# Output products of a batch put together in a fused diffusion, attention, expert and low-rank kernel, with a rebuilt start and waits tile by tile

## The chip, the core and the metric

The kernel runs on one core of a Trainium2 chip. The metric is the device time of one execution in microseconds (us), as the median of several runs. The core has a matrix engine (TensorE, PE in the profile; PEld is its loading of the stationary operand), a vector engine (VectorE, DVE), a scalar engine (ScalarE, ACT), a general engine (GpSimd, POOL) and a queue that issues most transfers (SyncE, SP). Each engine works through its own list of instructions in order, and waits on semaphores for the others. SBUF is the working memory of 128 partitions; PSUM holds the results of TensorE, in banks of 128 x 512 values (the kernel lays out eight).

## What is computed

Eight batches of 512 x 512 values go through four layers. All is float32.

```python
x = diffuse(x, A, B, dt)       # L0: max(f + df * dt, 0); df from first and second
                               #     differences of A*f and B*f, one-sided at the borders
x = attention_block(x, ...)    # L1: layernorm scaled by an embedding of the time step,
                               #     16 heads of 32, with a bias and a mask; then an MLP of 2048
x = expert_ffn(x, eidx)        # L2: weights of the expert eidx[b]: gelu MLP, + x, layernorm,
                               #     * gamma[e] + beta[e]
feats = (x @ basis) @ basis.T[:, :32]
strength = sigmoid(relu(mean(x) @ gate_w1.T + gate_b1) @ gate_w2.T + gate_b2) * sigmoid(safety)
out = x + strength * (feats @ resp_w.T + resp_b + safety_bias)     # L3
```

## The kernel before

`fused_kernel` (L40) runs three stages one after another. P = 128 is the number of partitions, R = 4 the number of row groups of a batch (a batch is held as 128 partitions x 4 rows x 512), and RK = 32 the rank of L3. Instructions wrapped in `pin` keep the order of the program text on their engine, so this order is written out by hand.

**The grid stage** (`grid_stage`, L215 to L517) computes L0 of batch 0, and the border values ("edges") of all batches. At the start `rows_in` loads A, B and x in half blocks on the SP queue (L274). Then SP issues the weights of the embedding (`load_wada`), Wq, Wk, Wv and Wo (`load_w`, L168) and the small bias rows (`load_rows`). VectorE multiplies coefficients with x (ca, cb, cc, ce, cg, then e, g, c, ga, gb, q, t, all at L237); TensorE adds the shifted products up in four accumulators l, by multiplying with shifted identity matrices zi (L243). POOL brings in the border rows: `edge_in` issues, behind a copy of x named gate_e (L312), transfers of edge_f into fe (64 partitions) and, per side, a broadcast of edge_c into ec, eight broadcasts in all. The coefficients also go to DRAM as coef_q, coef_e and so on (L386), for the other batches. Then come the embedding product pe on TensorE (L148), the row blocks x = relu(l * dth + f) for r = 0, 3, 1, 2, and after all four the transfers x<-xe that put the border values of batch 0 in place (two on SP, two on ACT). The statistics ln_st of the layernorm (L499) follow, for rows 0 and 3 after those transfers; the normalised x (L511) and the scale ada (L157) release the next stage.

**The attention stage** (`attention_stage`, L521 to L1105) goes through 128 units (b, c, r): batch, group of four heads, row group. Its start, before the loop, is at L1042 to L1065: loads of masks (`mask_in`: mu, L564), of biases (`load_bias`: bt) and of the next batch's grid data (`grid_loads`: gf, gq), the transposes of x (`x1_in`: xtr, L546), the products pq (L543), `grid_early` (gq times gf on VectorE, L663), the products pk and pv, and the scores s (L543). The scores of four heads lie on four groups of 32 rows of TensorE, and go to four banks. The grid of batches 1 to 7 is computed by VectorE inside the loop.

**The MLP stage** (`mlp_stage`, L1109 to L1769) makes 16 passes q: 0 to 7 the MLP of L1, 8 to 15 the experts. A pass has its products cut in a Strassen-like way: 4 groups of 7 products u with the first weights, at steps 0 to 27, then 7 products y with the second weights that begin at steps 28, 32, 36, 40, 44, 48 and 52 and take 4 steps each. `at(hooks, s, f, ...)` runs f behind step s; so all other work is threaded in by hand. All matmuls of this stage have the line of a helper, L1137; additions on VectorE have L1143, those on POOL L1146.

In passes 9 to 15 the batch before (o = q - 1) gets its L3: `tail_norm` at step 8, `tail_turn` at 29 to 35, `tail_gamma` 37, `tail_feats` 38, `gate` 39, `strength` 41, `add_beta` 42 (x + beta on POOL), and `tail_out` for the four row groups r behind steps 49, 51, 53 and 55 (50 to 53 in pass 15):

```python
def tail_sum(q, r):                       # L1643
    po = ps.tile([P, D], F32, tag="u" if last else "tr", bufs=6 if last else 2)
    mm(po, ft[m, :], rw[m, :], True, not last)      # m: rows 32r to 32r+31
def tail_add(q, r):                       # L1653
    # x[:, r] = po * strength + x[:, r] on VectorE (L1656); behind odd r the store to out
```

Row group r of po stands on TensorE's rows 32r to 32r + 31. PSUM tiles come from two sets: "u", six banks, for the products u and y, and "tr", two banks, for transposes and small products. The last batch (o = 15) has its L3 after the loop (L1741 to L1769), with its four po one after another in the text, in the set "u".

A pool of tiles (`tile_pool`) that is opened where a closed pool has lain waits at its first use for what used that memory before. All pools of the kernel are opened without an option for this.

Of the kernel before, what the change touches and what calls it, by code (L numbers as in the profile page):

```python
# [11 lines left out]
F32 = mybir.dt.float32  # L12
# [12 lines left out]
R = 4  # L25
# [14 lines left out]
def fused_kernel(ctx: ExitStack, tc: tile.TileContext, a: dict):  # L40
# [64 lines left out]
    freq = ep.tile([P, 2], F32, name="freq")  # L105
    nc.scalar.dma_start(freq, a["c_freq"])
    bada = ep.tile([P, 2 * KC], F32, name="bada")
    nc.scalar.dma_start(bada, a["b_ada"])
    nc.scalar.dma_start(sigs, a["safety"][None, :].to_broadcast([P, NB]))
    nc.scalar.dma_start(eidx, a["eidx"][None, :])  # L110
    nc.vector.tensor_scalar(bada[:, 0:KC], bada[:, 0:KC], 1.0, None, ALU.add)
    tf = ep.tile([P, NB], F32, name="tf")
# [25 lines left out]
    nc.scalar.activation(sc, sc, AF.Silu)  # L138
    nc.scalar.activation(sigs, sigs, AF.Sigmoid)

    def embed(ps):
# [11 lines left out]
        return pe  # L153

    def embed_out(pe):
        tc.keep_in_program_order(
            nc.vector.tensor_tensor(  # L157
                ada, pe, bada[:, :, None].to_broadcast([P, 2 * KC, NB]), ALU.add
            )
        )  # L160
# [3 lines left out]

    def load_w():
        for n in ("Wq", "Wk", "Wv", "Wo"):
            w[n] = w8(wo8, n)
            nc.sync.dma_start(w[n], a[n].rearrange("(k p) m -> p k m", p=P))  # L168

# [3 lines left out]

    def load_rows():
        nc.sync.dma_start(bqk[:, 0, :], a["bq"])
# [4 lines left out]
    grid = grid_stage(  # L180
        tc, a, const, small, dram, xt[0], mhalf, ident, load_wada, load_w, load_rows, embed,
        embed_out,
    )


    io = ctx.enter_context(tc.tile_pool(name="io", bufs=1))
    g2 = const.tile([P, 2, KC], F32, name="g2")
    nc.scalar.dma_start(g2[:, 0, :], a["g2"])
    nc.scalar.dma_start(g2[:, 1, :], a["beta2"])
    b1 = const.tile([P, NJ], F32, name="b1")  # L190
    nc.scalar.dma_start(b1, a["b1"])
    wl3 = const.tile([P, KC, RK], F32, name="wl3")
    x1d = [dram.tile([P, R, D], F32, name=f"x1d_{b}") for b in range(NB)]
    first = attention_stage(
        tc, a, small, xp, xt, x_home, x1d, grid, ident, sc1, shift, io, wo8, w, (bqk, bvc, bo),
        g2, mhalf,
    )
# [17 lines left out]
def grid_stage(  # L215
    tc, a, const, small, dram, x, mhalf, ident, load_wada, load_w, load_rows, embed,
    embed_out,
):
# [26 lines left out]
    with ExitStack() as ctx:  # L245
# [21 lines left out]
        ec = gp.tile([N, 12, W + 2], F32, name="ec")  # L267
        pin(nc.gpsimd.memset(ec, 0.0))
        pin(nc.gpsimd.memset(fe, 0.0))
# [6 lines left out]
        with tc.tile_pool(name="raw", bufs=1) as rp:  # L276
# [3 lines left out]

            def edge_in(i, k):
                lo, hi = max(0, W * k - 1), min(D, W * k + W + 1)
                u = slice(lo - W * k + 1, hi - W * k + 1)
                p0 = n * i
                pin(nc.gpsimd.dma_start(fe[p0 : p0 + n, :, u], a["edge_f"][:, :, lo:hi]))
                for side in range(2):
                    p1 = p0 + side * NB
                    pin(
                        nc.gpsimd.dma_start(
                            ec[p1 : p1 + NB, :, u],  # L290
                            a["edge_c"][side : side + 1, :, lo:hi].to_broadcast([NB, 12, hi - lo]),
                        )
                    )

# [7 lines left out]
            rows_in(b2, a["B"][2])  # L302
            nc.scalar.dma_start(gw, a["c_ghost"].to_broadcast([P, 16]))
            nc.scalar.dma_start(dth, a["dt"][None, :].to_broadcast([P, NB]))
            load_wada()
            load_w()
            load_rows()
# [5 lines left out]
            for i, k in enumerate(blocks):  # L313
                edge_in(i, k)

# [9 lines left out]

        wp = ctx.enter_context(tc.tile_pool(name="l0", bufs=1))
        acc = [ps.tile([P, D], F32, name=f"l0_{r}") for r in range(R)]
# [53 lines left out]
        for m, w, o in (  # L381
            ("q", b2, 1), ("e", ce, 1), ("c", cc, 0), ("g", cg, 1), ("a", ca, 0), ("b", cb, 0)
        ):
# [92 lines left out]
        pin(nc.vector.tensor_scalar(xe, xe, 0.0, None, ALU.max))  # L476
        xed = dram.tile([n, D], F32, name="xed")
        for i, k in enumerate(blocks):
            pin(nc.gpsimd.dma_start(xed[:, W * k : W * k + W], xe[n * i : n * i + n, :]))
        pe = embed(ps)  # L480
        pin(nc.vector.tensor_scalar(dth, dth, 0.5, None, ALU.mult))
        st = small.tile([P, R, 6], F32, name="ln0_st", tag="ln0_st", bufs=1)
        mv = small.tile([P, R, 2], F32, name="ln0_mv", tag="ln0_mv", bufs=1)
        for r in (0, 3, 1, 2):
            stt(x[:, r, :], acc[r], dth[:, 0:1], f[:, r, :], ALU.mult, ALU.add)
            pin(nc.scalar.activation(x[:, r, :], x[:, r, :], AF.Relu))
        for o, u, c in ((0, 3 * n, 0), (n, n, 2 * W)):
            for side, q_ in ((0, nc.sync), (1, nc.scalar)):
                p, r = side * (P - 1), side * (R - 1)
                e0 = o + side * NB  # L490
                pin(
                    q_.dma_start(
                        x[p : p + 1, r, c : c + 2 * W].rearrange("o (b w) -> o b w", w=W),
                        xe[e0 : e0 + u + 1 : u, :],
                    )
                )

# [23 lines left out]
def attention_stage(  # L521
    tc, a, small, xp, xt, x_home, x1d, grid, ident, sc1, shift, io, wo8, w, rows,
    g2, mhalf,
):
# [10 lines left out]
    with ExitStack() as ctx:  # L535
        wp = ctx.enter_context(tc.tile_pool(name="aw", bufs=1))
        pp = ctx.enter_context(tc.tile_pool(name="ap", bufs=2))
        ps = ctx.enter_context(tc.tile_pool(name="a_ps", bufs=1, space=PSUM))

# [340 lines left out]
        def grid_early(j):  # L880
            grid_sums(1, j)
            grid_loads(1, j)
# [163 lines left out]
        grid_loads(1, -2)  # L1046
        load_bias(*units[0])
        grid_loads(1, -1)
        mask_in(0, 1)
        load_bias(*units[1])  # L1050
        for c in range(KC):
            x1_in(0, c)
        mask_out(0, 0)
        pin(nc.scalar.copy(bvr, bvc[:, :, None].to_broadcast([P, KC, P])))
        add_mask(*units[0])
        drain(q_block(0, 0))
        grid_early(0)
        grid_early(1)
# [3 lines left out]
        mask_in(0, 2)  # L1062
        mask_in(0, 3)
        grid_early(2)
        scores(*units[0])  # L1065
# [43 lines left out]
def mlp_stage(tc, a, small, xp, io, wo8, x1d, ident, eidx, sigs, layernorm, rstd_of, phalf, wl3, g2, b1, first):  # L1109
# [19 lines left out]
    with ExitStack() as ctx:  # L1129
        wp = ctx.enter_context(tc.tile_pool(name="fw", bufs=1))  # L1130
        ap = ctx.enter_context(tc.tile_pool(name="fa", bufs=2))
        ps = ctx.enter_context(tc.tile_pool(name="f_ps", bufs=2, space=PSUM))
        dp = ctx.enter_context(tc.tile_pool(name="x2_dram", bufs=1, space=bass.MemoryType.DRAM))
# [509 lines left out]
        def tail_sum(q, r):  # L1643
            last = q == NQ - 1
            ft, m = outs[q]["ft"], slice(r * RK, (r + 1) * RK)
            po = outs[q]["po", r] = ps.tile(
                [P, D], F32, name=f"po_{q}_{r}", tag="u" if last else "tr", bufs=6 if last else 2
            )
            mm(po, ft[m, :], rw[m, :], True, not last)
            if last:  # L1650
                mm(po, ones[m, :], rb[m, :], False, True)

        def tail_add(q, r):  # L1653
# [6 lines left out]
            if r % 2:  # L1660
# [21 lines left out]
        for q in range(NQ):  # L1682
# [36 lines left out]
            elif q > NB:  # L1719
# [138 lines left out]
```

## Time and profile before

| | us |
|---|---|
| median of 3 runs | 2807.26 (2805.81 to 2810.29) |
| profiled execution | 2809.32 |
| its span | 2807.5 |
| VectorE busy | 1942.0 |
| ScalarE busy | 1002.8 |
| GpSimd busy | 1503.9 |
| software queue q0 (POOL's transfers) | 3680 packets, 11.07 MB |

The span is what the profile covers; the execution's own time is 1.8 us longer. The mean granted clock of TensorE is 0.991 of full speed. The grid stage with the start of attention takes about the first 80 us; the attention loop goes on to 1143 us, and the MLP stage to the end.

How to read the profile: "y<-wo,act" is an instruction by the names of its output and inputs; "L1137" is its line in the kernel; "128x512 f32" is its shape and type. "x16" counts instructions. The chain is followed back from the last instruction of a window: each piece is a stretch of work, or a transfer, that released the next. A line of waits tells which engine's instruction waited for whose. A float32 matmul shows as two or four instructions, one for each pass.

### The profile page before, as it was taken

To read this page: it belongs to the slowest core of one execution; us is meant where nothing else is said; L and a number is where in the kernel's file an instruction comes from. 1 tells how busy PE (TensorE), PEld (TensorE's weight loads), DVE (VectorE), ACT (ScalarE), POOL (GpSimd) and SP (SyncE) were. 2 spreads that over 40 slices of the span, in tenths; PEclk is the share of its full clock that TensorE was granted. 3 is DMA by queue.
4 is the path that set the end of the run, shared out by engine and by line. 5 is a ranking of instruction groups with operands and counts; after the bars stand their busy time and mean duration, and the time that the engine had idled before them with its cause. 6 is when DMAs were issued, how large, how long until landed. Compare 5 with 4: busy or idle time off the path is not lost.

```text
span 2807.5 us, 39790 instructions
## 1 busy us (share of the span) xinstructions
PE 2729.1 (97%) x14654; PEld 2011.6 (72%) x14654; DVE 1942.0 (69%) x3581; ACT 1002.8 (36%) x2133; POOL 1503.9 (54%) x1081
## 2 busy tenths in 40 slices
PE   5999999999999998999999999999999999999998
PEld 3455555555555554788888888888888888888886
DVE  6888898988888766576666756655466556556554
ACT  1466666666666666212111211211121121121221
POOL 3455555555555654466566655656456545535633
PEclk9999999999999999999999999999999999999998
DMA  9665657566666554542533444253223133143120
GB/s 300 225 204 180 235 172 241 186 223 214 194 233 191 157 160 158 181 121 49 158 124 83 109 143 124 49 169 120 73 97 125 59 137 128 42 154 113 42 75 31
DMA packets 190400, 405.62 MB, mean 144 GB/s; under 512 B 24104, under 2 KB 28784, under 8 KB 183934
## 3 DMA queue, kind: packets, MB, share of 16 engines
q1 hardware_dynamic: 185192, 391.93, 42.2%
q0 software_dynamic: 3680, 11.07, 3.2%
q8 instruction: 117, 1.92, 0.3%
q14 instruction: 77, 0.63, 0.1%
q10 hardware_dynamic: 1334, 0.07, 0.0%
HBM read 367.32 MB, written 31.50 MB: 142 GB/s over the span
## 4 chain that ended last, share of the span: by engine, by line
PE 86%; DVE 9%; ACT 2%; DMA 2%; issue 1%; SPq 0%; DVEq 0%; ACTq 0%; POOL 0%
PE y L1137 28%; PE u L1137 28%; PE tr L546 6%; PE s L543 4%; PE ctx L543 4%; PE o L543 3%; PE pv L543 3%; PE pq L543 3%; PE pk L543 2%; DVE bt L973 2%; DVE x L663 2%; DVE pt L998 1%; DMA Wo<-in_Wo 1%; ACT bt L978 1%; PE po L1137 1%; PE btr L1140 1%
## 5 line engine op out<-in xcount | busy, mean ns | idle before, releaser
L1137 PE MATMUL y<-wo,act 128*128 128x256 f32 x2560 | 578.9, 381 | 0.0
L950 POOL TENSOR_TENSOR bt<-bt,mk 128x1024 f32<-128x1024 f32 x256 | 543.2, 2142 | 64.2 <-DMA bt<-in_bias 61.2
L1137 PEld LDWEIGHTS y<-wo,act 128*128 128x128 f32 x2560 | 479.4, 190 | 82.2 <-issue 20.6
L978 ACT ACTIVATE bt<-bt,mn 128x512 f32<-128x512 f32 x512 | 365.4, 715 | 115.5 <-DVE mn L973 115.4
L546 PEld LDWEIGHTS tr<-ident,bt 128*128 128x128 f32 x2048 | 228.2, 141 | 167.7 <-issue 115.7
L1137 PE MATMUL u<-bt,wi 128*128 128x256 f32 x1440 | 330.5, 379 | 0.0
L973 DVE CUSTOM_DVE_ANT_0 bt<-s,bt 128x512 f32<-128x512 f32 x512 | 330.4, 682 | 0.0
L1143 DVE TENSOR_TENSOR act<-u,u 128x512 f32<-128x512 f32 x256 | 173.3, 686 | 209.9 <-PE u L1137 132.6
L1137 PEld LDWEIGHTS u<-bt,wi 128*128 128x128 f32 x1440 | 273.5, 190 | 37.2
L546 PE MATMUL tr<-ident,bt 128*128 128x128 f32 x2048 | 279.9, 278 | 18.8 <-DVE pt L998 7.7
L998 DVE COPY pt<-tr 128x512 f32<-128x512 f32 x256 | 175.8, 687 | 113.3 <-PE tr L546 113.0
L1137 PE MATMUL u<-tb,ws 128*128 128x256 f32 x1024 | 242.1, 379 | 0.0
L1137 PE MATMUL y<-t,s 128*128 128x256 f32 x1024 | 234.2, 380 | 0.0
L1000 ACT COPY pt<-tr 128x512 f32<-128x512 f32 x256 | 148.1, 579 | 183.1 <-PE tr L546 180.7
L1137 PEld LDWEIGHTS u<-tb,ws 128*128 128x128 f32 x1024 | 194.4, 190 | 26.5
L1146 POOL TENSOR_TENSOR t<-wo,t 128x512 f32<-128x512 f32 x64 | 104.5, 1647 | 200.5 <-PE y L1137 200.5
L1137 PEld LDWEIGHTS y<-t,s 128*128 128x128 f32 x1024 | 191.1, 190 | 24.1
L1457 ACT ACTIVATE act<-act,b 128x512 f32<-128x512 f32 x128 | 82.9, 711 | 292.4 <-DVE act L1143 292.4
L1457 ACT ACTIVATE act<-act,bi 128x512 f32<-128x512 f32 x128 | 83.8, 713 | 282.6 <-DVE act L1143 282.6
L1143 DVE TENSOR_TENSOR x<-y,x 128x512 f32<-128x512 f32 x96 | 64.5, 685 | 159.0 <-PE y L1137 105.1
L543 PE MATMUL s<-kt,qt 32*128 32x512 f32 x1024 | 171.7, 645 | 2.3 <-DVE mn L973 1.4
L1143 DVE TENSOR_TENSOR u<-u,u 128x512 f32<-128x512 f32 x192 | 131.3, 684 | 58.8 <-PE u L1137 58.8
(314 smaller groups left out, 4283.5 us busy)
## 6 DMA issues: line engine op xcount, KB each, us to landing
bt<-in_bias SPq DMA_DIRECT2D x256, 512.0 KB
wo<-in_W SPq DMA_DIRECT2D x32, 1024.0 KB
wi<-in_Wi SPq DMA_DIRECT2D x32, 1024.0 KB
wo<-in_Wo_e SPq DMA_DIRECT2D x32, 1024.0 KB
wi<-in_W SPq DMA_DIRECT2D x28, 1024.0 KB
gq<-coef_q SPq DMA_DIRECT2D x21, 512.0 KB
x1d<-x SPq DMA_DIRECT2D x8, 1024.0 KB
x<-x1d SPq DMA_DIRECT2D x8, 1024.0 KB
```

Source lines behind the costliest of these rows:

```text
L543: pin(nc.tensor.matmul(out, lhsT=lhsT, rhs=rhs, start=start, stop=stop))
L546: pin(nc.tensor.transpose(out, src, ident))
L663: pin(nc.vector.tensor_tensor(out, x, y, op))
L950: nc.gpsimd.tensor_tensor(bt, bt, mask[b, r][:, None, :].to_broadcast([P, 2, S]), ALU.add)
L973: nc.vector.tensor_tensor_reduce(bt[:, i, :], ss[h], bt[:, i, :], -1.0, 3.0e38, ALU.add, ALU.min, mn)
L978: nc.scalar.activation(bt[:, i, :], bt[:, i, :], AF.Exp, bias=mn, scale=-1.0, accum_out=sums[b, c, r][:, h : h + 1],)
L998: pin(nc.vector.tensor_copy(pt[:, :, r % 2, :], tr))
L1000: pin(nc.scalar.copy(pt[:, :, r % 2, :], tr))
L1137: pin(nc.tensor.matmul(out, lhsT=lhsT, rhs=rhs, start=start, stop=stop))
L1143: pin(nc.vector.tensor_tensor(out, x, y, op))
L1146: pin(nc.gpsimd.tensor_tensor(out, x, y, op))
L1457: nc.scalar.activation(acts[g][:, k, :], acts[g][:, k, :], func, bias=bi[:, j : j + 1])
```

## The change

Three things change.

*The tail.* po always takes a bank of the set "u". `tail_out` is gone; in passes 9 to 15 all four `tail_sum` run behind step 45, and the four `tail_add` behind steps 47, 48, 49 and 51.

*The start.* The edge coefficients come by four small transfers into a tile of 8 partitions (ec8), issued first on POOL; four matmuls with a selector (sel8) spread them to 64 partitions in PSUM, and ACT copies them to ec. Small loads (b_ada, eidx, gw, dth, safety) move from the ACT queue to SP, g2, beta2 and b1 to a later place on SP; the sigmoid of safety comes first on ACT. Of the attention weights only Wq and Wk are loaded early; Wv goes behind the first unit's bias, Wo behind the second's. The addition of 1 to b_ada goes behind the embedding product. The transfers x<-xe are issued behind row blocks 0 and 3, and those of xed move from POOL to the ACT queue. The store order of coef_c and coef_g is swapped. `grid_early(0)` stands ahead of the first `mask_out`, `add_mask` and `q_block`.

*The pools.* Eight pools (io, l0, aw, ap, a_ps, fw, fa, f_ps) get `reuse_waits="tile"`: the wait for what lay in the memory before is made for each tile by itself.

```diff
-                [P, D], F32, name=f"po_{q}_{r}", tag="u" if last else "tr", bufs=6 if last else 2
+                [P, D], F32, name=f"po_{q}_{r}", tag="u", bufs=6
-        def tail_out(q, rows):
-            for r in rows:
-                tail_sum(q, r)
-                tail_add(q, r)
...
                 for r in range(R):
-                    at(hooks, (50 + r) if q == NQ - 1 else (49 + 2 * r), tail_out, o, [r])
+                    at(hooks, 45, tail_sum, o, r)
+                    at(hooks, (47, 48, 49, 51)[r], tail_add, o, r)
```

```diff
+            for i, k in enumerate(blocks):
+                c, u = edge_cols(k)
+                pin(nc.gpsimd.dma_start(ec8[2 * i : 2 * i + 2, :, u], a["edge_c"][:, :, c]))
+            pin(nc.gpsimd.tensor_copy(
+                sel8, ident[0 : N // NB, 0 : N // NB, None].to_broadcast([N // NB, N // NB, NB])))
...
-            load_w()
+            load_w("Wq", "Wk")
...
             for i, k in enumerate(blocks):
-                edge_in(i, k)
+                c, u = edge_cols(k)
+                pin(nc.gpsimd.dma_start(fe[n * i : n * i + n, :, u], a["edge_f"][:, :, c]))
+            for i in range(4):
+                pec = ps.tile([N, 3, W + 2], F32, name=f"pec_{i}", tag="pec", bufs=2)
+                mm(pec, sel8.rearrange("q s b -> q (s b)"), ec8[:, 3 * i : 3 * i + 3, :], True, True)
+                pin(nc.scalar.copy(ec[:, 3 * i : 3 * i + 3, :], pec))
...
-        wp = ctx.enter_context(tc.tile_pool(name="l0", bufs=1))
+        wp = ctx.enter_context(tc.tile_pool(name="l0", bufs=1, reuse_waits="tile"))
...
         pe = embed(ps)
+        embed_bias()
...
         for r in (0, 3, 1, 2):
             stt(x[:, r, :], acc[r], dth[:, 0:1], f[:, r, :], ALU.mult, ALU.add)
             pin(nc.scalar.activation(x[:, r, :], x[:, r, :], AF.Relu))
-        for o, u, c in ((0, 3 * n, 0), (n, n, 2 * W)):
...
+            if r == 3:
+                edges()
+        xed = dram.tile([n, D], F32, name="xed")
+        for i, k in enumerate(blocks):
+            pin(nc.scalar.dma_start(xed[:, W * k : W * k + W], xe[n * i : n * i + n, :]))
```

```diff
         load_bias(*units[0])
+        load_w("Wv")
         grid_loads(1, -1)
         mask_in(0, 1)
         load_bias(*units[1])
+        load_w("Wo")
         for c in range(KC):
             x1_in(0, c)
+        grid_early(0)
         mask_out(0, 0)
         pin(nc.scalar.copy(bvr, bvc[:, :, None].to_broadcast([P, KC, P])))
         add_mask(*units[0])
         drain(q_block(0, 0))
-        grid_early(0)
```

More of the change, by code (lines that the diff above doesn't have):

```diff
@@ L106, in fused_kernel @@
     nc.scalar.dma_start(freq, a["c_freq"])
+    nc.sync.dma_start(sigs, a["safety"][None, :].to_broadcast([P, NB]))
+    nc.scalar.activation(sigs, sigs, AF.Sigmoid)
     bada = ep.tile([P, 2 * KC], F32, name="bada")
[L108 to L111, printed above, removed]
     tf = ep.tile([P, NB], F32, name="tf")
@@ L138, in fused_kernel @@
     nc.scalar.activation(sc, sc, AF.Silu)
-    nc.scalar.activation(sigs, sigs, AF.Sigmoid)
     def embed(ps):
@@ L153, in embed, with embed_bias @@
         return pe
+    def embed_bias():
+        tc.keep_in_program_order(
+            nc.vector.tensor_scalar(bada[:, 0:KC], bada[:, 0:KC], 1.0, None, ALU.add)
+        )
     def embed_out(pe):
@@ L163, in fused_kernel, with load_w @@
     w = {}
-    def load_w():
-        for n in ("Wq", "Wk", "Wv", "Wo"):
+    def load_w(*names):
+        for n in names:
             w[n] = w8(wo8, n)
-            nc.sync.dma_start(w[n], a[n].rearrange("(k p) m -> p k m", p=P))
+            tc.keep_in_program_order(
+                nc.sync.dma_start(w[n], a[n].rearrange("(k p) m -> p k m", p=P))
+            )
     bqk = const.tile([P, 2, KC], F32, name="bqk")
@@ L174, in load_rows @@
     def load_rows():
+        nc.sync.dma_start(bada, a["b_ada"])
+        nc.sync.dma_start(eidx, a["eidx"][None, :])
         nc.sync.dma_start(bqk[:, 0, :], a["bq"])
@@ L181, in fused_kernel, with load_late @@
         tc, a, const, small, dram, xt[0], mhalf, ident, load_wada, load_w, load_rows, embed,
-        embed_out,
+        embed_bias, embed_out,
     )
-    io = ctx.enter_context(tc.tile_pool(name="io", bufs=1))
+    io = ctx.enter_context(tc.tile_pool(name="io", bufs=1, reuse_waits="tile"))
     g2 = const.tile([P, 2, KC], F32, name="g2")
-    nc.scalar.dma_start(g2[:, 0, :], a["g2"])
-    nc.scalar.dma_start(g2[:, 1, :], a["beta2"])
     b1 = const.tile([P, NJ], F32, name="b1")
-    nc.scalar.dma_start(b1, a["b1"])
+    def load_late():
+        for t, v in ((g2[:, 0, :], "g2"), (g2[:, 1, :], "beta2"), (b1, "b1")):
+            tc.keep_in_program_order(nc.sync.dma_start(t, a[v]))
     wl3 = const.tile([P, KC, RK], F32, name="wl3")
@@ L195, in fused_kernel @@
         tc, a, small, xp, xt, x_home, x1d, grid, ident, sc1, shift, io, wo8, w, (bqk, bvc, bo),
-        g2, mhalf,
+        g2, mhalf, load_w, load_late,
     )
@@ L216, in grid_stage @@
     tc, a, const, small, dram, x, mhalf, ident, load_wada, load_w, load_rows, embed,
-    embed_out,
+    embed_bias, embed_out,
 ):
@@ L267, in grid_stage @@
         ec = gp.tile([N, 12, W + 2], F32, name="ec")
-        pin(nc.gpsimd.memset(ec, 0.0))
         pin(nc.gpsimd.memset(fe, 0.0))
@@ L279, in grid_stage, with edge_cols @@
             )
-            def edge_in(i, k):
+            ec8 = rp.tile([N // NB, 12, W + 2], F32, name="ec8")
+            sel8 = rp.tile([N // NB, N // NB, NB], F32, name="sel8")
+            pin(nc.gpsimd.memset(ec8, 0.0))
+            def edge_cols(k):
                 lo, hi = max(0, W * k - 1), min(D, W * k + W + 1)
[L283 to L293, printed above, removed]
+                return slice(lo, hi), slice(lo - W * k + 1, hi - W * k + 1)
+            for i, k in enumerate(blocks):
+                c, u = edge_cols(k)
+                pin(nc.gpsimd.dma_start(ec8[2 * i : 2 * i + 2, :, u], a["edge_c"][:, :, c]))
+            pin(
+                nc.gpsimd.tensor_copy(
+                    sel8, ident[0 : N // NB, 0 : N // NB, None].to_broadcast([N // NB, N // NB, NB])
+                )
+            )
             halves = slice(0, 2), slice(2, 4)
@@ L302, in grid_stage @@
             rows_in(b2, a["B"][2])
-            nc.scalar.dma_start(gw, a["c_ghost"].to_broadcast([P, 16]))
-            nc.scalar.dma_start(dth, a["dt"][None, :].to_broadcast([P, NB]))
+            nc.sync.dma_start(gw, a["c_ghost"].to_broadcast([P, 16]))
+            nc.sync.dma_start(dth, a["dt"][None, :].to_broadcast([P, NB]))
             load_wada()
-            load_w()
+            load_w("Wq", "Wk")
             load_rows()
@@ L313, in grid_stage @@
             for i, k in enumerate(blocks):
-                edge_in(i, k)
+                c, u = edge_cols(k)
+                pin(nc.gpsimd.dma_start(fe[n * i : n * i + n, :, u], a["edge_f"][:, :, c]))
+            for i in range(4):
+                pec = ps.tile([N, 3, W + 2], F32, name=f"pec_{i}", tag="pec", bufs=2)
+                mm(
+                    pec, sel8.rearrange("q s b -> q (s b)"), ec8[:, 3 * i : 3 * i + 3, :],
+                    True, True,
+                )
+                pin(nc.scalar.copy(ec[:, 3 * i : 3 * i + 3, :], pec))
             for h in halves:
@@ L381, in grid_stage @@
         for m, w, o in (
-            ("q", b2, 1), ("e", ce, 1), ("c", cc, 0), ("g", cg, 1), ("a", ca, 0), ("b", cb, 0)
+            ("q", b2, 1), ("e", ce, 1), ("g", cg, 1), ("c", cc, 0), ("a", ca, 0), ("b", cb, 0)
         ):
@@ L476, in grid_stage @@
         pin(nc.vector.tensor_scalar(xe, xe, 0.0, None, ALU.max))
-        xed = dram.tile([n, D], F32, name="xed")
-        for i, k in enumerate(blocks):
-            pin(nc.gpsimd.dma_start(xed[:, W * k : W * k + W], xe[n * i : n * i + n, :]))
         pe = embed(ps)
+        embed_bias()
         pin(nc.vector.tensor_scalar(dth, dth, 0.5, None, ALU.mult))
@@ L483, in grid_stage, with edges @@
         mv = small.tile([P, R, 2], F32, name="ln0_mv", tag="ln0_mv", bufs=1)
+        def edges():
+            for o, u, c in ((0, 3 * n, 0), (n, n, 2 * W)):
+                for side, q_ in ((0, nc.sync), (1, nc.scalar)):
+                    p, r = side * (P - 1), side * (R - 1)
+                    e0 = o + side * NB
+                    pin(
+                        q_.dma_start(
+                            x[p : p + 1, r, c : c + 2 * W].rearrange("o (b w) -> o b w", w=W),
+                            xe[e0 : e0 + u + 1 : u, :],
+                        )
+                    )
         for r in (0, 3, 1, 2):
@@ L486, in grid_stage @@
             pin(nc.scalar.activation(x[:, r, :], x[:, r, :], AF.Relu))
-        for o, u, c in ((0, 3 * n, 0), (n, n, 2 * W)):
[L488 to L496, printed above, removed]
+            if r == 3:
[3 more added lines that the diff above has]
+            pin(nc.scalar.dma_start(xed[:, W * k : W * k + W], xe[n * i : n * i + n, :]))
         def stats(r):
@@ L522, in attention_stage @@
     tc, a, small, xp, xt, x_home, x1d, grid, ident, sc1, shift, io, wo8, w, rows,
-    g2, mhalf,
+    g2, mhalf, load_w, load_late,
 ):
@@ L535, in attention_stage @@
     with ExitStack() as ctx:
-        wp = ctx.enter_context(tc.tile_pool(name="aw", bufs=1))
-        pp = ctx.enter_context(tc.tile_pool(name="ap", bufs=2))
-        ps = ctx.enter_context(tc.tile_pool(name="a_ps", bufs=1, space=PSUM))
+        wp = ctx.enter_context(tc.tile_pool(name="aw", bufs=1, reuse_waits="tile"))
+        pp = ctx.enter_context(tc.tile_pool(name="ap", bufs=2, reuse_waits="tile"))
+        ps = ctx.enter_context(tc.tile_pool(name="a_ps", bufs=1, space=PSUM, reuse_waits="tile"))
         pin = tc.keep_in_program_order
@@ L1063, in attention_stage @@
         mask_in(0, 3)
+        load_late()
         grid_early(2)
@@ L1129, in mlp_stage @@
     with ExitStack() as ctx:
-        wp = ctx.enter_context(tc.tile_pool(name="fw", bufs=1))
-        ap = ctx.enter_context(tc.tile_pool(name="fa", bufs=2))
-        ps = ctx.enter_context(tc.tile_pool(name="f_ps", bufs=2, space=PSUM))
+        wp = ctx.enter_context(tc.tile_pool(name="fw", bufs=1, reuse_waits="tile"))
+        ap = ctx.enter_context(tc.tile_pool(name="fa", bufs=2, reuse_waits="tile"))
+        ps = ctx.enter_context(tc.tile_pool(name="f_ps", bufs=2, space=PSUM, reuse_waits="tile"))
         dp = ctx.enter_context(tc.tile_pool(name="x2_dram", bufs=1, space=bass.MemoryType.DRAM))
```

## The prediction

> **What bounds the kernel now.** I read the page's busy shares and chain first. The chain is the path that ended last, and TensorE (PE) holds 86% of it:
>
> ```profile
> PE 2729.1 (97%) x14654; PEld 2011.6 (72%) x14654; DVE 1942.0 (69%) x3581; ACT 1002.8 (36%) x2133; POOL 1503.9 (54%) x1081
> PE 86%; DVE 9%; ACT 2%; DMA 2%; issue 1%; SPq 0%; DVEq 0%; ACTq 0%; POOL 0%
> ```
>
> So a microsecond leaves in two ways only: less TensorE work, or TensorE not waiting. The change tries one of each, and I read one view for each. First the chain of waits in pass q=12 (start, length, work):
>
> ```profile
> 2441.92 3.46 PE y L1137 x16
> 2445.38 1.05 PE po L1137 x2
> 2446.43 3.65 PE y L1137 x16
> 2450.08 1.05 PE po L1137 x2
> ```
>
> TensorE has no gap here. An output product po (two matmuls on 32 rows) takes 1.05 us, and the sixteen y behind it take 3.65 instead of 3.46 us: 1.05 + 0.19 = 1.24 (single starts give 1.248). Four stand in each of seven passes.
>
> Second the chain through the first 78 us, cut to its long pieces:
>
> ```profile
> 26.67 34.86 DMA Wo<-in_Wo
> ...
> 61.56 3.29 DMA x<-xe
> ...
> 65.32 3.54 DMA gf<-in_x
> 68.86 0.91 DVE x L511 x2
> ...
> 70.00 3.42 PE xtr L546 x16
> 73.42 3.45 PE pq L543 x8
> ...
> 77.56 4.28 DVE gq L663 x2
> ```
>
> Here transfers hold the end. The list of waits has the same from the engines (total, times, longest):
>
> ```profile
> PE l L243 <- DVE e L237: 26.6, 1, 26.6
> DVE ln_st L499 <- DMA x<-xe: 7.6, 1, 7.6
> PE xtr L546 <- DVE ada L157: 6.6, 1, 6.6
> DVE qe L237 <- DMA ec<-in_edge_c: 1.6, 1, 1.6
> DVE ca L237 <- DMA a<-in_A: 1.0, 1, 1.0
> ```
>
> TensorE waits 26.6 us for its first operand, works without a gap to 63.4 (timeline), then waits 6.6 us for a layernorm, whose last rows come by the edge transfers x<-xe.
>
> **The tail.** All four po of a batch move behind step 45, their adds to steps 47 to 51. Nothing is taken from the arithmetic; the question is whether four po cost four times one. Where row groups lie side by side, the timeline has (start, length, group):
>
> ```profile
> 81.07 1.14 PE L543 MATMUL s<-kt,qt 32*128 32x512 f32 x8 [0.78 <-ACT kt L632]
> 82.14 14.00 PE L543 MATMUL pv<-Wv,x 128*128 128x512 f32 x32
> ```
>
> Eight matmuls, the same size as po's, four row groups in four banks: the next work starts 1.07 us later. Four po would thus cost what one costs, plus 0.02. The last batch has its po together already, 1.87 us start to start for eight, at half clock: the same. Here the Trainium skill speaks a little against it: "TensorE: Matmul & The Clock Gate", Part 3, Measured speedup, gives a packing of four row groups 3.07 times, not 4. By that a group costs 4 × 1.05 / 3.07 = 1.37 us, by the row 1.07; over seven passes 2 us. I take the row, and leave the 2 us to the range. Saving per pass: 3 × 1.248 − 0.02 = 3.72. Passes 9 to 14: 6 × 3.72 = 22.3. In pass 15 one of the four bothers little work behind it (4.85 us for the four, 1.27 after; 3.6), and its split tail_norm has three adds put ahead of it on VectorE; its first transposes at step 51 have 3 us of room for 2.5 us, so I take off 0.3: 3.3. Sum **25.6 us**.
>
> What hides the rest. "TensorEngine Tiling (Array Packing)", PSUM Bottleneck, warns that the array gets faster while banks are emptied no faster: four adds at 0.75 us are 3.0 us on VectorE, all due within 4 steps, where before they lay 4.7 us apart. VectorE is idle for 5.34 us before 2443.69 there, the place that the first add moves into, so I cost them at nothing; without that cover it would be up to 3.0 us a pass. po now takes four of the six banks of the ordinary products. In the new order of instructions these are banks whose products were read some 4 us and more before; the product of step 48 gets the bank read at 2435.9, the one of step 52 that of the product of step 44. The latter is the only close one: 6.9 us of TensorE work lie between. POOL's x + beta (2433.28, 4.52 us) ends at 2437.8, about 1.3 us before the first add can start. The two out stores now both go ahead of the next experts' Wo on SP; that is needed 18 steps later. Nothing.
>
> **The front, up to the first transposes (xtr at 70.0).** (1) VectorE's first grid product comes about 1.5 us earlier: the + 1 on b_ada, which waited at 7.4 for a small transfer, is gone from ahead. I estimate the waits for halves of a and b (1.0 + 0.4 + 0.2) go too, as small loads leave the early queue. Together 3.1, so e reaches TensorE at 23.4 instead of 26.5. Bounds: 1 and 3.5. The order then is TensorE-bound: its first group took 6.40 us at a cold clock, later ones 3.60, and that stays; embed ends at 63.4 − 3.1 = 60.3. (2) The eight broadcast transfers of the edge coefficients become four small ones, four matmuls and four ACT copies. No row has these matmuls; by 1.05 us for a 512-wide pair they are 4 × 0.8 = 3 us, while TensorE still idles before e (it idles 23 us): nothing. From the other side, if ec8 came late they would stand ahead of the first l on TensorE's queue and hold it; ec8 is now issued first on POOL, so I expect it within 10 us. The 1.6 us wait of qe goes, and 10 us of narrow packets (172 to 216 GB/s between 30 and 40 us, 420 later) thin out. (3) Wv and Wo go behind the first biases: 2.1 MB, 5 us at 410 GB/s, leave the way of eidx and the edge rows. (4) The edge transfers go out after row blocks 0 and 3. x rows start 4.2 us earlier (3.1 and part of the 1.6), r=3 is done near 50.5, the transfers (3.29) land near 54, against 64.85. The statistics then run straight behind the others: 54.2 plus the 5.0 us from 64.76 to 69.77 gives 59.2. So TensorE, not the norm, is last: xtr at 60.3 + 0.1, that is **9.6 us** earlier, and the 6.6 us hole is closed.
>
> What is late next: the attention loads. SP issues mu at 64.93 now, behind one wait on all earlier transfers; tile by tile it needs only its own, about 54, 10 us earlier; so gf and gq keep pace. Wv now lands near 70, needed near 72 (82.14 − 10): 2 us of room, Wo later still. The gq products (4.28 us) move from after qt into 3.25 us of VectorE idle before it: 2.1 us more, bounds 0 and 3. The changed waits also touch the start of the MLP stage, where TensorE waits 0.9 us: 0.5. Front sum 9.6 + 2.1 + 0.5 = **12.2 us**, bounds 7 and 16: between 80 and 200 us TensorE idles only some 7 us more than in the steady part, and VectorE is the busy engine up to 130, so part may be given back.
>
> **Total.** 25.6 + 12.2 = 37.8. Span 2807.5 − 37.8 = 2769.7; 1.8 us lie around it: 2771.5 against the profiled 2809.3. The median stands 2.1 below that run: 2769.4, say **2769.5**.
>
> **Rivals.**
> A. Front given back. Earlier xtr helps only if VectorE's backlog (masks, gq, bt of the next batch) and the loads move along. With Wv and Wo behind biases, TensorE could wait at pv or o. Then 4 of 12 remain: 2777.5. For: VectorE-bound to 130 us. Against: its load starts 10 us earlier too. 0.18.
> B. The four po run one after another in this place. Then only the disturbed y (0.19 three times) is saved, 4 us in all: 2807.3 − 4 − 12.2 = 2791. Against: both rows above. 0.06.
> C. The change doesn't do what it says: the front's waits by tile meet another late transfer, and TensorE still waits till 70. 2807.3 − 25.6 = 2781.5. 0.04.
> D. Slower: VectorE's own order. The first add stands ahead of x_add(p3), and waits for POOL's x + beta. If POOL is late, p3 keeps its bank and step 52 stalls. POOL may end 11 us later before TensorE feels it (y_52 starts at 2450.1, less 0.75 and 0.69 for the two adds, less 2437.8); each us beyond costs 7. The 37.8 us are gone at 5.4 us of stall a pass, 11 + 5.4 = 16.4 us late; at 18 late it is 2807.3 − 37.8 + 49 = 2818. Against: nothing in the change moves POOL there. 0.04.
> About 0.02 is left for within 0.2% (5.6 us), roughly what a measurement of this kernel can tell from no change.
>
> **How the numbers follow.** My forecast has 0.66, A 0.18, B 0.06, C 0.04, D 0.04, no change 0.02. The forecast's own range: the group by the skill's price (+2), front 16 (−4) or 7 (+5): 2764 to 2775. To leave out no more than 2 in 10 it reaches over most of A: 2763 to 2779. Faster 0.66 + 0.18 + 0.06 + 0.04 = 0.94, same 0.02, slower 0.04.
>
> **What would show it.** Tail: one group of po x8 of about 1.1 us per pass, and y x16 of 3.46 on both sides but the one behind; if po spreads over 4 us, B. A wait of y for VectorE at step 52 is D. Front: e at about 23.4, xtr at about 60.3 waiting for TensorE's own embed; x<-xe landing near 54; a wait of pv for Wv or of o for Wo would be A; xtr near 70, C. It is wrong if the saving does not split about two to one between tail and front.

## The result and the profile after

The changed kernel takes 2773.36 us (2770.04 to 2773.65, four runs) against 2808.3 us of the kernel before, run beside it; the ratio is 0.9872, with a 95% interval of 0.9858 to 0.9885. A second series of the same kernel gave 2770.72 against 2808.7, ratio 0.9865 (0.9848 to 0.9881). The forecast was 2769.5, with a range of 2763 to 2779: right in direction and close in size, some of it for other reasons than it gave.

The profiled execution has a span of 2771.4 us, 36.2 less than before. First, the page's busy shares and chain:

```profile
PE 2708.5 (98%) x14662; PEld 2009.6 (73%) x14662; DVE 1941.1 (70%) x3581; ACT 1004.9 (36%) x2137; POOL 1501.9 (54%) x1074
PE 86%; DVE 10%; ACT 3%; DMA 1%; issue 1%; SPq 0%; ACTq 0%; POOL 0%; DVEq 0%
```

TensorE is busy for 20.6 us less: the tail saves it about 25 (below), and the new selector matmuls cost it 5.4. The share of transfers in the chain has gone from 2% to 1%. The chain in pass q=12 (start, length, work):

```profile
2412.01 3.46 PE y L1164 x16
2415.46 0.44 PE btr L1167 x4
2415.90 1.07 PE po L1164 x8
2416.97 3.65 PE y L1164 x16
```

All eight po matmuls stand in 1.07 us, and one block of y behind them is disturbed (3.65 instead of 3.46), where there were four of each. TensorE's timeline at the start (start, length, group, and in brackets the idle time ahead of it):

```profile
13.27 5.43 PE L251 MATMUL pec<-ec,sel 8*64 8x390 f32 x8 [13.27 <-DMA ec<-in_edge_c]
23.00 5.12 PE L251 MATMUL l<-e,zi 128*128 128x512 f32 x8 [4.31 <-DVE e L245]
...
42.59 7.03 PE L251 MATMUL l<-t,zi 128*128 128x512 f32 x16
49.46 10.21 PE L145 MATMUL pe<-sc,wada 128*128 128x8 f32 x64
59.52 3.65 PE L570 MATMUL xtr<-ident,x 128*128 128x128 f32 x16
62.97 3.85 PE L567 MATMUL pq<-x,Wq 128*128 128x512 f32 x8
```

The hole of 6.6 us ahead of xtr is gone: xtr starts at 59.52 instead of 70.00, straight behind the embedding product pe. The list of waits says who is last now:

```profile
PE l L251 <- DVE e L245: 4.3, 1, 4.3
DVE ada L159 <- PE pe L145: 0.9, 1, 0.9
```

VectorE waits for TensorE's embedding before it can make ada, and xtr no longer waits for ada: it starts at 59.52, ahead of it.

```profile
59.71 0.22 DVE L159 TENSOR_TENSOR ada<-pe,bada 128x64 f32<-128x64 f32 x1 [0.88 <-PE pe L145]
```

To see where the 36.2 us come from, I put the starts of the same instructions of both traces side by side: the first u of each pass of the MLP stage. The second pass starts 10.95 us earlier, and the tenth also 10.95 (all passes in between take the same time to 0.01 us). From there each of passes 9 to 14 takes 103.80 instead of 107.53 us, 3.73 less, and the rest from pass 15 on 127.33 instead of 130.20, 2.87 less. 10.95 + 6 × 3.73 + 2.87 = 36.2.

### The profile page after: what moved, and what is told of

Its sections match the earlier page's. It is cut to its first block, busy times and chain, and to the rows that moved or that the text cites. A ratio compares the mean times of both kernels' runs of the same rounds, so it can differ in the third digit from the quotient of the medians.

```text
span 2771.4 us, 39819 instructions
## 1 busy us (share of the span) xinstructions
PE 2708.5 (98%) x14662; PEld 2009.6 (73%) x14662; DVE 1941.1 (70%) x3581; ACT 1004.9 (36%) x2137; POOL 1501.9 (54%) x1074
## 4 chain that ended last, share of the span: by engine, by line
PE 86%; DVE 10%; ACT 3%; DMA 1%; issue 1%; SPq 0%; ACTq 0%; POOL 0%; DVEq 0%
PE u L1164 28%; PE y L1164 28%; PE tr L570 7%; PE s L567 4%; PE ctx L567 4%; PE o L567 3%; PE pv L567 3%; PE pq L567 3%; PE pk L567 2%; DVE bt L997 2%; DVE x L687 2%; DVE pt L1022 1%; ACT bt L1002 1%; PE btr L1167 1%; PE ytr L1167 1%
## 5 line engine op out<-in xcount | busy, mean ns | idle before, releaser
L1164 PEld LDWEIGHTS u<-bt,wi 128*128 128x128 f32 x1440 | 273.5, 190 | 37.2
```

Of the source, the lines that this page charges most:

```text
L1164: pin(nc.tensor.matmul(out, lhsT=lhsT, rhs=rhs, start=start, stop=stop))
```

## Experiments

Twelve runs follow, in three sets; each set has a chip of its own and its own runs of the kernel before, from which the ratios are taken. The starts of single instructions are taken from each kernel's trace:

| kernel | median, us | ratio (95%) | first xtr | first s | third s after first s | first u after last s | first u |
|---|---|---|---|---|---|---|---|
| before | 2808.3 | | 70.00 | 81.07 | 29.1 | 29.44 | 1143.34 |
| changed | 2773.36 | 0.9872 (0.9858 to 0.9885) | 59.52 | 71.03 | 27.4 | 28.40 | 1131.96 |
| changed, again | 2770.72 | 0.9865 (0.9848 to 0.9881) | 59.43 | 71.94 | 26.7 | 28.40 | 1128.41 |
| tail alone | 2783.89 | 0.9911 (0.9894 to 0.9927) | 69.14 | 80.94 | 28.5 | 29.44 | 1144.02 |
| start alone | 2796.55 | 0.9959 (0.9945 to 0.9973) | 59.61 | 71.64 | 26.9 | 28.40 | 1134.60 |
| po one by one | 2799.09 | 0.9964 (0.9952 to 0.9977) | 59.66 | 71.12 | 27.7 | 28.40 | 1129.49 |
| po two by two | 2781.86 | 0.9906 (0.9889 to 0.9922) | 59.61 | 71.85 | 26.9 | 28.40 | 1128.54 |
| pools as before | 2774.94 | 0.9879 (0.9862 to 0.9895) | 60.38 | 72.46 | 29.9 | 29.44 | 1135.70 |
| Wv, Wo early | 2769.18 | 0.9860 (0.9844 to 0.9877) | 59.62 | 70.60 | 27.2 | 28.40 | 1126.16 |
| edges last | 2772.71 | 0.9869 (0.9853 to 0.9885) | 59.77 | 71.51 | 27.5 | 28.40 | 1133.53 |
| gq in old place | 2772.66 | 0.9871 (0.9855 to 0.9888) | 59.76 | 71.68 | 27.8 | 28.40 | 1133.04 |
| broadcasts back | 2774.37 | 0.9877 (0.9860 to 0.9893) | 58.73 | 71.09 | 28.1 | 28.40 | 1133.03 |
| ec8 alone | 2803.93 | 0.9982 (0.9972 to 0.9993) | 64.05 | 74.97 | 29.0 | 29.44 | 1137.16 |
| combined | 2771.97 | 0.9871 (0.9855 to 0.9888) | 60.51 | 71.94 | 26.3 | 28.40 | 1130.17 |

The last column must be read with care: the first u of one and the same program (changed, start alone, and the two with other tails differ only behind it) falls anywhere from 1128.4 to 1134.6 ("The changed kernel again" shows where that comes from). So differences of 2 or 3 us in the medians are not read; the columns ahead of it repeat to about 0.2 us (xtr) and 1 us (s). With the old start, xtr lies 0.9 us apart in two traces (before and tail alone).

### Tail alone

The kernel before with

```diff
-                [P, D], F32, name=f"po_{q}_{r}", tag="u" if last else "tr", bufs=6 if last else 2
+                [P, D], F32, name=f"po_{q}_{r}", tag="u", bufs=6
...
-                    at(hooks, (50 + r) if q == NQ - 1 else (49 + 2 * r), tail_out, o, [r])
+                    at(hooks, 45, tail_sum, o, r)
+                    at(hooks, (47, 48, 49, 51)[r], tail_add, o, r)
```

> The kernel before with the new tail alone (four output products together behind step 45 in banks of the set u, adds at 47 to 51), the old start and the old waits. My theory, that four row groups in four banks cost what one costs and nothing else matters: 3.73 us less in each of passes 9 to 14 and 2.9 in pass 15, so 25.3 us below the kernel before (2808.3), about 2783; pass to pass 103.8 us instead of 107.5. Rival, that part of the tail's gain came through the new waits of the last stage's pools: the passes stay above 104.5 and the time above 2787.

Measured: 2783.89, 24.9 us below the kernel before; passes 9 to 14 take 103.80 us. The theory holds, and the tail's gain needs nothing of the pools' option.

### Start alone

The changed kernel with the same lines turned back.

> The changed kernel with the old tail (one output product behind every second step, in the set tr). My theory, that start and tail add up: first transposes at 59.5, MLP stage about 11 us earlier than in the kernel before, passes 9 to 14 at 107.5 us each; 10.9 us below 2808.3, about 2797.4. Rival, that the earlier start is partly lost when the tail is slow: above 2801.

Measured: 2796.55, 12.3 us below; xtr at 59.61, and passes of 107.53. The two parts add up: 24.9 + 12.3 = 37.2, against 34.9 and 38.0 for both together in two series. The 12.3 is known no better than that: three of the five runs lie at 2795.5 to 2796.6, with a granted clock of 0.994, and two at 2800.4 and 2801.7, with 0.992.

### The four po one by one

```diff
-                    at(hooks, 45, tail_sum, o, r)
+                    at(hooks, 45 + r, tail_sum, o, r)
```

> The changed kernel with its four output products one by one behind steps 45, 46, 47 and 48, same banks, same adds. My theory, that only standing side by side on TensorE saves time: each breaks into the ordinary products by itself again, 3 x 1.25 us more in each of seven passes, so about 2773 + 25 = 2798, passes at 107.5. Rival, that the six banks of the set u instead of the two of tr, or the earlier place, gave the gain: it stays near 2773 with passes at 103.8.

Measured: 2799.09, and passes that gain 0.00 us. The chain in pass q=12:

```profile
2424.61 1.05 PE po L1164 x2
2425.66 1.93 PE y L1164 x8
2427.59 1.05 PE po L1164 x2
```

Same banks, nearly the same place, same adds, and the whole gain of the tail is gone. Each po costs 1.05 us, and the eight y behind it take 1.93 where eight take 1.73 undisturbed (half of 3.46).

### The four po two by two

```diff
-                    at(hooks, 45, tail_sum, o, r)
+                    at(hooks, 45 + r // 2, tail_sum, o, r)
```

> The changed kernel with its output products two by two, behind steps 45 and 46. If a group costs about 1.25 us whatever its number of row groups, two groups cost 1.25 us more than one in each of seven passes: 2773 + 8.7 = 2782, passes at 105.05. If instead the overlap of two is poorer or better than that of four (a cost that grows with the number), the passes lie off 105.05 by over 0.3 us.

Measured: 2781.86, passes of 105.04 us, 2.49 us less than one by one. The chain in pass q=12:

```profile
2416.22 1.06 PE po L1164 x4
2417.28 1.92 PE y L1164 x8
2419.20 1.06 PE po L1164 x4
2420.26 1.92 PE y L1164 x8
```

One, two or four row groups take 1.05, 1.06 and 1.07 us: what counts is how often the products y are interrupted, not how many po stand in one place. Four, two and one of them give 0, 2.49 and 3.73 us.

### Pools as before

`reuse_waits="tile"` taken from all eight pools of the changed kernel.

> The changed kernel with its eight pools as before, so that a pool's first use waits for all that lay in its memory. First transposes in the four runs with the new start: 59.5 to 59.7 us; first scores 71.0 to 71.9; third scores 26.9 to 27.7 after the first; first u of the MLP stage 28.4 after the last scores. My theory, that the waits by tile let the attention loads go out at 53 instead of behind the last edge store near 59, and close the hole ahead of the MLP stage: mask and grid loads leave SP about 6 us later, the first scores stay within 2 us of 71 (TensorE sets them), the third scores come 2 to 6 us later, the u 29.4 after the last scores; in all 3 to 8 us over 2773. Rival, that the new order of loads does it and the pools' option nothing: all milestones within 0.5 us.

Measured: 2774.94. SP's first mask load leaves at 56.15, 3.3 us later than the 52.83 of the changed kernel; Wv, queued behind it, comes late:

```profile
60.38 3.65 PE L570 MATMUL xtr<-ident,x 128*128 128x128 f32 x16 [0.36 <-issue]
...
74.87 0.67 PE L567 MATMUL pv<-Wv,x 128*128 128x512 f32 x1 [1.27 <-DMA Wv<-in_Wv]
```

and ada on VectorE:

```profile
60.05 0.22 DVE L159 TENSOR_TENSOR ada<-pe,bada 128x64 f32<-128x64 f32 x1 [0.40 <-PE pe L145]
```

All the milestones that the waits could touch are later: xtr by 0.9, the third s by 4 in all (1.4 + 2.5), the first u of the MLP stage by 1.04. The rival falls: the milestones show it, while the median alone (1.6 and 4.2 us above the two series of the changed kernel) would not. SP's loads came 3 us later, not the 6 that I gave.

The 0.9 us at xtr has two parts. Here xtr starts 0.10 us behind the end of ada, and so it does in all four traces without waits by tile; in all ten with them it starts 0.41 us ahead of that end, right behind pe. So about 0.5 us is a wait for ada that the option takes away. The rest is pe, which ends at 60.02 instead of 59.67.

### Wv and Wo early

```diff
-            load_w("Wq", "Wk")
+            load_w("Wq", "Wk", "Wv", "Wo")
...
-        load_w("Wv")
...
-        load_w("Wo")
```

> The changed kernel with Wv and Wo loaded behind Wk again, 2.1 MB ahead of the small rows. By my forecast they take 5 us out of the way of the edge transfers. If so, x<-xe and the statistics come up to 5 us later, and the first transposes, which have 0.9 us of room there, come at 60 to 64. Rival, that the queue has room by then anyway (transfers at 0.66 to 0.73 of their time between 30 and 40 us): first transposes within 0.3 us of 59.6.

Measured: xtr at 59.62, within 0.1 us. The rival holds: in this kernel the 2.1 MB are not in the way of xtr. The median, 2769.18, is the lowest of all; see "combined" and "The changed kernel again".

### Edge transfers last

```diff
-            if r == 3:
-                edges()
+        edges()
         xed = dram.tile([n, D], F32, name="xed")
```

> The changed kernel with the edge transfers issued behind all four row blocks again. The two blocks that now follow cost ScalarE 1.2 us, so the transfers go out 1.2 us later, the layernorm ends at 60.0 instead of 58.8, behind the embedding product (59.7): first transposes 0.3 to 0.5 us later. Rival, that ScalarE, which now waits 2 us with the last two blocks behind its own transfers, is better off without: no later, or earlier.

Measured: xtr at 59.77, behind pe as before. The layernorm's last step on VectorE:

```profile
53.19 0.69 DVE L522 BATCH_NORM_STATS2 ln_st<-x 128x6 f32<-128x512 f32 x1 [0.70 <-DMA x<-xe]
56.28 1.92 DVE L534 TENSOR_SCALAR x<-x,ln_mv,ln_r 128x512 f32<-128x512 f32 x4 [1.17 <-POOL ln_r L531]
```

It ends at 58.20; in the changed kernel at 58.83, and 59.38 in its repeat. So issuing the edges earlier did not help: it makes ScalarE hold back its last two row blocks by the 2.04 us that its own two issues take, and the statistics wait for those. The rival holds.

### The products gq in their old place

`grid_early(0)` back behind `q_block(0, 0)`.

> The changed kernel with the first grid products of the next batch (gq times gf, 2.5 us) back behind the first mask, bias and q block. The prediction put 2.1 us on this move. If that holds, the first or third scores come about 2 us later. My view from the trace of the changed kernel is now that TensorE sets the first scores, and VectorE idles 4.4 us before 72.0 waiting for coef_e, where these products fit: both within 0.5 us.

Measured: the first s at 71.68, within what five traces with the move show (71.0 to 71.9). The third s comes at 99.5, against 98.4 to 98.8 there; by the ninth nothing of this is left (151.2 against 150.1 to 151.2). So the 2.1 us that the prediction put on this move are not there.

### Broadcasts back, and ec8 alone

By then I thought that the eight broadcasts of edge_c had jammed the transfers. Two kernels: the changed one with `edge_in` and its broadcasts in place of ec8, and the kernel before with ec8, sel8 and the four matmuls in place of `edge_in`'s broadcasts.

> The changed kernel with the edge coefficients by eight broadcasts from DRAM again (no ec8, no selector matmuls). My theory now, that these broadcasts with their narrow packets are what fills the transfer engines between 30 and 45 us, holds SP's issues and makes the edge transfers late: VectorE waits for ec again (1 to 2 us), x<-xe goes out 3 to 10 us later than 49, first transposes at 62 to 68 instead of 59.6, and the first l group takes 6.3 instead of 5.1 us, since nothing has warmed TensorE's clock. Rival, that the order of the loads and the waits by tile suffice: first transposes at 61 or earlier, with the 1.2 us of the colder clock as all that is lost.

> The kernel before with the new edge coefficients alone (four small transfers, selector matmuls, copies by ScalarE). If the broadcasts jam the transfers, SP no longer stands 14.5 us at bo, x<-xe goes out some 5 to 10 us before 60.7, and the first transposes come at 62 to 66 instead of 70. Rival, that Wv and Wo or the late eidx hold SP: x<-xe within 2 us of 60.7, first transposes at 68 or later.

Measured: xtr at 58.73 with the broadcasts back, earlier than without; and at 64.05 with ec8 alone, 6 us before the kernel before. The first falls against my theory, the second for it. SP's queue shows how both can be. The kernel before (start, time in issuing):

```profile
26.67 5.68 SPq L168 DMA_DIRECT2D Wo<-in_Wo  x1
32.40 5.80 SPq L175 DMA_DIRECT2D bqk<-in_bq  x1
38.25 0.89 SPq L176 DMA_DIRECT2D bqk<-in_bk  x1
39.18 0.43 SPq L177 DMA_DIRECT2D bvc<-in_bv  x1
39.66 14.48 SPq L178 DMA_DIRECT2D bo<-in_bo  x1
60.72 1.38 SPq L492 DMA_DIRECT2D x<-xe  x2
```

With ec8 alone, the broadcasts gone, Wv and Wo still early:

```profile
34.17 3.45 SPq L178 DMA_DIRECT2D bo<-in_bo  x1
53.84 2.19 SPq L503 DMA_DIRECT2D x<-xe  x2
```

With the broadcasts back in the changed kernel, Wv and Wo late:

```profile
31.06 3.91 SPq L184 DMA_DIRECT2D bo<-in_bo  x1
48.55 1.96 SPq L496 DMA_DIRECT2D x<-xe  x2
```

In the kernel before, SP stands at bo (256 KB, one row spread over 128 partitions) from 39.7 to 54.1; then it reads eidx, eight values up to 60.6, and only at 60.7 can it issue its edge transfers, whose data and row block are ready at 54.1. Take away the broadcasts, or the weights that were ahead of bo, and bo takes under 4 us. "Wv, Wo early" shows the third corner: these loads early, but no broadcasts, and no stall (bo 1.23 us). So in these kernels the stall comes only with both. That the broadcasts are needed is shown by one change alone (ec8). For the weights it is not as clean: the kernel with the broadcasts back has the rest of the new start too, such as other small loads on SP.

SP was not the only one. ScalarE's queue issues the other two edge transfers:

```profile
55.48 6.66 ACTq L492 DMA_DIRECT2D x<-xe  x2
```

The first leaves at 55.48, the second only at 61.56. It waits on the semaphore that Wo's transfer counts up, whose last piece lands at 61.54, and its own landing at 64.85 is the last of the four. In "tail alone", which has the same start, Wo lands at 59.83 and this transfer leaves at 59.85. With ec8 alone, Wo lands at 42.20 and holds nothing. So Wo, which was on its way for 35 us while the broadcasts ran, held the edges as well, as the chain of the kernel before says; an SP that was free would have left this one where it was.

What is left for ec8 in the whole: VectorE waits for ec at most 0.25 us in the changed kernel and in the one with the broadcasts back.

The broadcast kernel's median is 3.7 us above the changed kernel's beside it, with an earlier xtr. Its loss lies in the attention stage (first u at 1133.03 against 1128.41). Of these 4.6 us, 3.0 fall between units 112 and 127 and are the scatter that "The changed kernel again" explains; whether the rest belongs to the kernel stays open.

### Combined

Wv and Wo early, the edges last, and each selector matmul made twice (`for _ in range(2): mm(pec, ...)`).

> The changed kernel with three things on top: Wv and Wo early, the edge transfers behind all four row blocks, and the four selector matmuls each made twice (the second writes the same values), so that TensorE is busy up to e. If TensorE's clock is what makes the first l group 5.1 to 6.3 us long, it takes 3.6 to 4.2, and the embedding product ends 1 to 2 us earlier; the layernorm ended at 58.2 where the edges went last, so first transposes at 58.3 to 59. Time 2766 to 2770. If the group stays above 5 us, the clock is not the cause.

Measured: 2771.97, and 2770.72 for the changed kernel beside it: not better, with xtr at 60.51, where 58.3 to 59 was expected (the doubled matmuls hold back l to 23.96). So the low median of "Wv, Wo early" did not carry over to this version of it. TensorE's timeline:

```profile
13.41 10.62 PE L251 MATMUL pec<-ec,sel 8*64 8x390 f32 x16 [13.41 <-DMA ec<-in_edge_c]
23.96 5.07 PE L251 MATMUL l<-e,zi 128*128 128x512 f32 x8
```

TensorE worked without a gap for 10.6 us ahead of l, and the first group was slow all the same. Its first three starts lie 0.85 to 1.01 us apart, the others 0.43 to 0.47. In the other thirteen traces the slow stretch of that group is 2.8 to 5.8 us long, here 2.8. That the clock makes it slow can be read from the traces: in all fourteen the first record of a full clock begins within the group, where its starts close up (here at 26.75). So it is the second way out: these matmuls, on 8 rows, do not raise the clock. They too start 0.65 us apart for 390 columns, where 0.43 us for 512 columns would give 0.33. A kernel with wide matmuls in their place, which would prove it, was not run.

### The changed kernel again

> The changed kernel as it is, on the same chip as the three others, to set them against: 2770 to 2774. If the version with early weights is better by a real amount, the combined one is at least 3 us below this.

Measured: 2770.72, with the same program as 2773.36. The traces are alike up to 1070 us but for one stretch near 150; then the granted clock (the column behind POOL) differs:

```profile
1075.00:1085.00 10.00, 9.90 (x58) 4.79 (x58) 3.82 (x11) 4.42 (x12) 5.01 (x3) 0.72 0.27 78
```

```profile
1075.00:1085.00 10.00, 8.47 (x61) 4.96 (x52) 6.79 (x18) 7.59 (x18) 7.27 (x5) 1.00 0.44 135
```

The first is the changed kernel's first trace, the second its repeat. Between units 112 and 127 the one takes 111.6 us and the other 108.7.

The other traces go the same way. Where the clock is at half for no time between 1070 and 1100 us, these units take 108.74 us (three traces, "Wv, Wo early" among them); with 3.41 us at half they take 110.4 (one), with 6.83 us 111.6 to 111.9 (nine), and with 10.24 us 113.2 ("start alone"). That is most of the scatter of the first u, and of the low median of "Wv, Wo early". What decides whether such a stretch comes is not shown.

## Why the prediction was right

**The tail, by its own steps.** Right in mechanism and size. A group of four costs 1.07 us, as the row of the scores said; the price of the Trainium skill ("TensorE: Matmul & The Clock Gate", Part 3, Measured speedup: 3.07 times) would, as an estimate, have given 1.37 us, and 3.42 us a pass instead of 3.72; measured are 3.73. The cover of the adds on VectorE held: no y waits anywhere in these passes. The product of step 48 and that of step 52 find their banks free, so rival D has nothing to show. In pass 15 the term is 2.87, not 3.3 (this pass differs by 0.5 us between the changed kernel and its repeat): I took 0.3 us for the layernorm that now stands behind three adds, but the first transposes at step 51 cost more,

```profile
PEld ytr L1167 <- DVE x L85: 0.8, 2, 0.5
```

two waits of 0.8 us in all. Sum 25.2, predicted 25.6. Rival B (one after another) is what "po one by one" looks like: 0.00 instead of 3.73 a pass.

**The start, step (1).** e reached TensorE at 23.00, predicted 23.4. The waits for b and a did not all go (0.35 and 0.19 us remain), but VectorE began 2.5 us earlier, not 1.5. That the first l group stays at 6.40 was wrong: 5.12 here, 6.16 in the repeat. That pe takes 9.04 was wrong too, and on the other side: 10.21. The windows of the changed kernel show why:

```profile
50.00:55.00 5.00, 5.00 (x39) 5.00 (x39) 3.09 (x8) 1.15 (x2) 0.00 (x0) 0.82 0.61 198
55.00:60.00 5.00, 5.00 (x25) 5.00 (x26) 2.81 (x8) 0.00 (x0) 1.05 (x1) 0.50 0.78 292
60.00:65.00 5.00, 5.00 (x20) 3.93 (x20) 3.04 (x4) 2.52 (x4) 0.00 (x0) 0.65 0.87 273
```

The granted clock falls to 0.50 while TensorE is busy all the time with pe, 64 matmuls of 8 columns. It did so in the kernel before as well, but only after 59.4, for the last part of pe. That the two errors cancel is no chance: in all fourteen traces the clock is full for 27.31 us from its rise in the first l group to its fall in pe. What comes late at one end is won at the other, and from the first start of l to the end of pe it is 36.7 to 36.8 us in every trace. So the sum of this step, e plus a fixed time, was sound, though the prediction did not give this reason.

**Step (2), the new edge coefficients.** Free, as costed, though ec8 came at 13.27 and not within 10 us: TensorE and ScalarE were idle, and ec came in time. What the prediction had wrong is that it put nothing of the hole on this step. Made alone, it moves xtr from 70.00 to 64.05.

**Steps (3) and (4), Wv and Wo, and the edges after two row blocks.** The prediction took the hole for one of order and bandwidth: 5 us of transfers out of the way, edges issued sooner. Neither move matters to xtr in the changed kernel (59.62 and 59.77 without them, 59.52 with). Step (4) failed as a reason. Step (3) is half right: in the kernel before, Wo did hold one of the edge transfers, to 61.54, and with the broadcasts back it is the late weights, with the rest of the new start, that keep the hole closed; but with ec8 in place it adds nothing. The prediction did not see the second hold at all, SP standing for 14.5 us at bo. The size came out right, since the hole closes either way and xtr then follows pe. Of the 10.5 us (predicted 9.6) 6.3 are the hole (xtr stands 6.64 us behind the end of pe in the kernel before, 0.36 with ec8 alone), 3.6 the earlier e (23.00 instead of 26.58), and 0.5 the wait for ada that the waits by tile take away, which the prediction did not have.

**What comes behind.** The 2.1 us for gq are wrong: TensorE, not VectorE, sets the first s, and products moved into a hole of a waiting engine gained nothing. About as much came from elsewhere: the third s comes 26.7 to 27.7 us behind the first in five traces of the new start, 28.5 and 29.1 in two of the old, and one trace, "pools as before" with 29.9, puts that on the waits by tile. The 0.5 us at the MLP stage came as 1.04 less 0.44 that the first pass then loses (98.96 instead of 98.52), 0.6. Sum of the start in the profiled run 10.95, and 12.3 from the medians of "start alone", against 12.2. That these agree so well is in part luck, given the scatter. Rival A (given back later) did not happen: at unit 112 of the 128 the five traces are still 9.0 to 11.3 us ahead of the kernel before. Two small sums of the prediction are off, without weight: its bounds add up to 2765.5 to 2776.5, not 2764 to 2775, and rival C to 2781.7.

**What is left open.** The attention stage scatters by 3 us and more from run to run, so the start's gain is known to about that. Why the clock falls near 1075 us in most traces and not in all is not shown, and neither is how much of the stall at bo the late weights alone would have removed.

## What to carry to other kernels

A small product that breaks into a dense stream of matmuls costs by the interruption, not by its arithmetic: put those that lie on different row groups and in different banks side by side, and count interruptions before and after. When a chain names a large transfer, look at the issuing queues as well: an instruction that stands there may be a small load, both can hold the same work at once, and several unrelated changes can each free it, so test each alone before giving one the credit. Moving work into an engine's idle time gains only if that engine is last to release what follows.

## What the runs showed of the hardware

In all fourteen traces TensorE's clock falls to half while TensorE is busy without a gap, 3.7 to 5.2 us after pe begins, and the starts of pe go from 0.11 to 0.21 us apart. That the matmuls are narrow there (8 columns) is the likely reason; no run with wider ones tested it. Matmuls on 8 rows did not raise the clock in 10.6 us. The Trainium skill ("TensorE: Matmul & The Clock Gate", Part 1) has the clock released by about 3.4 us of sustained activity, in windows that run free of the program. The 2.8 to 5.8 us of the first wide group agree roughly, and the stretches at half that the traces hold, 3.41, 6.83 and 10.24 us, are one, two and three such windows; the two cases here say that busy time alone is not that activity. Free-running windows would also give what two runs of the same program show in the attention stage, where TensorE has small gaps: a stretch at 0.72 in one and 1.00 in the other, worth 2.9 us.
